# Which key tiles VectorE masks alone in a four-layer graph attention stack: second, sixth and eighth in place of third, sixth and eighth

## The chip, the cores and the metric

The kernel runs on one core of one Trainium2 chip. The metric is the device time of one execution in microseconds; the time before is the median of three runs.

## What is computed

The input is `x` of shape 16 x 1024 x 128 and one adjacency matrix of 1024 x 1024, with about one entry in 64 set. Three transformer layers follow each other and then one graph attention layer. One of the three, cut to what matters here:

```
Q, K, V = h @ Wq, h @ Wk, h @ Wv              # 8 heads of 16
scores  = Q K^T / sqrt(16); where adj == 0: -inf
attn    = softmax(scores) V
x = layer_norm(h + attn @ Wo + bo)
x = layer_norm(x + relu(x @ W1 + b1) @ W2 + b2)
```

The last layer adds a source and a destination score per edge, applies a leaky ReLU, masks, takes the softmax, sums the neighbours, adds the residual and normalises. The change touches only how the scores of the first three layers are masked.

## The kernel before, in words

**Blocks and steps.** A block is one batch element in one of the first three layers; there are 48, taken in groups of four batch elements (LANES, L655). A block has four *halves*: a group of four heads (g) and 512 of the queries (qh). A half has eight steps, one for each key tile of 128 keys, kt 0 to 7 in the code. So a block has 32 steps; they are numbered 0 to 31 below, and kt is the step modulo 8. The second, third, sixth and eighth key tile are kt 1, 2, 5 and 7.

**One step (score_step, L415).** TensorE computes the scores of two head pairs (pp 0 and 1), each into a PSUM buffer "s" of 128 x 1024 f32, of which there are three. Then each pair is masked and exponentiated, in one of two ways:

- The GpSimd way: ScalarE takes the exponential from PSUM into the tile `e` (L430), and GpSimd multiplies it by a 0/1 mask (L431). ScalarE frees the PSUM buffer.
- The VectorE way: VectorE adds a large negative number where there is no edge, from PSUM into `e` (L433), and ScalarE takes the exponential in place (L445). VectorE frees the PSUM buffer.

Pair 1 always goes the VectorE way. Pair 0 goes the GpSimd way, except at the key tiles in BOTH_ON_DVE (L37), where both go the VectorE way:

```
on_pool = pp == 0 and kt not in BOTH_ON_DVE
...
if on_pool:
    nc.scalar.activation(ev, psv, AF.Exp, scale=HD ** -0.5)
    behind["pool"] = nc.gpsimd.tensor_mul(ev, ev, m).ins
else:
    behind["dve"] = nc.vector.tensor_add(ev, psv, m).ins
    masked.append((2 * step_no[0] + pp + (kt not in BOTH_ON_DVE), ev))
```

A step of the second kind is called a *double step* below, and the others *mixed steps*. The list `masked` sets where ScalarE's in-place exponentials stand in its order (exponentials, L441): pair 0 of a double step in the same step, pair 1 of any step in the next one, behind that step's L430 if it is a mixed step.

**Four steps later (AHEAD, L36)** TensorE sums the values with `e` as weights into one PSUM buffer `acc` (av_step, L447; matmuls L450). With the last key tile of a half, which is summed in step 3 of the next half, finish (L453) transposes `acc` on VectorE into `tt` (L461). The first sum of the next half, in the step after, waits for that transposition, since `acc` has one buffer.

**The pieces.** All else is cut into pieces, at most one a step, put behind the step's scores and sums (piece, L691): the projections of the next block, and the output projection and feed-forward part of the block before. The table AT (L34) names the step of each piece. Pieces share one PSUM buffer "t". The second feed-forward product of the block before stands at steps 0 and 8, its output projection at 12 and 22; behind each of these come on VectorE an addition (L329), four bn_stats (L322) and four bn_aggr (L324), and on GpSimd the normalisation (L337 to L341). The splits of the projected keys and queries into a high and a low part (L385 on ScalarE, L386 on VectorE) stand at steps 9, 11, 14 and 17, the values' projection at 19 and 20. After the third layer of a batch element the pieces of the last layer (last_tasks, L541) ride in the same way, with edges (L607 on TensorE, L610 on VectorE) using the "s" buffers too.

**Orders.** In the main loop (L763) the order on TensorE and ScalarE is the program's own. On VectorE and GpSimd a planner orders the instructions ahead of time, by priority (the program's order, moved forward where soon(), L277, stands) among those that its own timing takes as ready; it also deals out the PSUM buffers. The transfers of SyncE are not touched by the change.

Of the kernel before, what the change touches and what calls it, by code (L numbers as in the profile page):

```python
# [33 lines left out]
AT = {"proj": (3, 6, 9, 11, 14, 17, 19, 20), "post": (12, 22, 23, 25, 26, 27, 28, 30, 32, 40, 41)}  # L34
AT_END = {3: (12, 21, 22, 24, 25, 26, 27, 28, 30, 31), 2: (8, 9, 13, 14, 15, 16, 17, 18, 20, 21)}
AHEAD = 4  # L36
BOTH_ON_DVE = (2, 5, 7)  # L37
TILES = {"w": 10, "x": LANES + 1, "last": 2}
BLOCKED = -57344.0

# [75 lines left out]
def fast_path(ctx: ExitStack, tc: tile.TileContext, a: dict, out: bass.AP, flag):  # L116
# [298 lines left out]
    def score_step(step):  # L415
# [3 lines left out]
        for pp in range(2):  # L419
# [6 lines left out]
            psv = ps.rearrange("p (r q) -> p r q", q=512)  # L426
            on_pool = pp == 0 and kt not in BOTH_ON_DVE
            m = (mask01 if on_pool else mask_add)[:, kt, q0:q0 + 512][:, None, :].to_broadcast([P, 2, 512])
# [3 lines left out]
# [3 lines that stand above are left out]
        step_no[0] += 1  # L435
# [616 lines left out]
```

## Time and profile before

| | |
|---|---|
| median of three runs | 3985.54 us (3984.45 to 3985.72) |
| the profiled execution's own time | 3983.09 us |
| its span, first to last instruction | 3981.2 us |
| mean granted TensorE clock | 0.987 |
| VectorE masks (L433) | 2112 of 1213 ns, 2493.6 us busy |
| ScalarE exponentials in place (L445) | 2112 of 1060 ns |
| ScalarE exponentials from PSUM (L430) | 960 of 1022 ns |
| GpSimd masks (L431) | 960 of 2026 ns |

A row of the timeline gives the start in microseconds, the busy time of the merged group, engine, line, operation, tiles written and read, and the count; a bracket at the end gives the engine's idle time ahead of it and what ended it. A row of the waits gives who waited for whom, the total in microseconds, the number of waits and the longest.

Measured from the first score matmul of one block to that of the next, 30 of the 48 blocks take 73.1 to 73.2 us and repeat the same pattern; they are called *plain blocks*. Most of the others carry pieces of the last layer and take 77 to 102 us; the first takes 82.5 us.

### The profile page before, as it was taken

How to read it: one execution, taken by the hardware profiler on the slowest of the kernel's cores; microseconds unless marked ns; L12 is line 12 of the kernel's file. 1: busy time of each engine (PE TensorE's matmuls, PEld its weight loads, DVE VectorE, ACT ScalarE, POOL GpSimd, SP SyncE). 2: the span in 40 equal slices, each digit the busy share in tenths (PEclk: the TensorE clock that was granted, in tenths of full speed). 3: DMA queues.
4: the chain of work that ended last, by engine and by line, in shares of the span. 5: the costliest groups of instructions: out<-in, count | busy, mean ns of one | idle time of the engine just before them, and what ended most of it. 6: DMA issues, size and time to landing. Idle time of an engine off the chain costs nothing.

```text
span 3981.2 us, 107823 instructions
## 1 busy us (share of the span) xinstructions
PE 3758.5 (94%) x44501; PEld 1558.5 (39%) x44501; DVE 3408.3 (86%) x5326; ACT 3392.8 (85%) x3961; POOL 3331.4 (84%) x3010
## 2 busy tenths in 40 slices
PE   7999999999999999999999999999999999999996
PEld 2333333344443333334444333333444433333345
DVE  7888988988888988988888898888888898898874
ACT  7999999977779999997777999999777799999860
POOL 4788888987789888988778888888877898898875
PEclk8999999999999999999999999999999999999998
DMA  6222222112222222222222222221222212222200
GB/s 163 65 65 53 55 65 63 46 48 65 56 58 57 65 65 54 54 65 55 55 55 55 65 53 56 65 64 45 55 55 55 71 46 62 65 51 58 66 8 20
DMA packets 124465, 233.13 MB, mean 59 GB/s; under 512 B 34624, under 2 KB 73792, under 8 KB 123968
## 3 DMA queue, kind: packets, MB, share of 16 engines
q1 hardware_dynamic: 123056, 225.74, 22.5%
q8 instruction: 354, 5.80, 0.6%
q14 instruction: 143, 1.17, 0.1%
q10 hardware_dynamic: 912, 0.42, 0.0%
HBM read 15.54 MB, written 8.39 MB: 6 GB/s over the span
## 4 chain that ended last, share of the span: by engine, by line
PE 61%; DVE 22%; POOL 9%; ACT 4%; issue 3%; SPq 0%; DMA 0%; DVEq 0%; ACTq 0%; POOLq 0%
PE acc L450 23%; PE t L297 19%; PE s L423 16%; DVE e L433 13%; POOL e L431 3%; POOL x L341 2%; PE t L286 2%; DVE lo L386 2%; DVE st L322 2%; ACT e L445 2%; ACT e L430 2%; DVE tt L461 1%; POOL mv L339 1%; PE s L297 1%; POOL x L345 1%
## 5 line engine op out<-in xcount | busy, mean ns | idle before, releaser
L433 DVE TENSOR_TENSOR e<-s,mask_add 128x1024 f32<-128x1024 f32 x2112 | 2493.6, 1213 | 344.6 <-PE s L423 263.7
L445 ACT ACTIVATE e<-e 128x1024 f32<-128x1024 f32 x2112 | 2203.4, 1060 | 206.1 <-DVE e L433 187.9
L431 POOL TENSOR_TENSOR e<-e,mask 128x1024 f32<-128x1024 f32 x960 | 1933.5, 2026 | 419.0 <-ACT e L430 419.0
L450 PE MATMUL acc<-e,v 128*17 128x512 f32 x12288 | 1627.8, 601 | 73.3 <-DVE tt L461 47.8
L423 PE MATMUL s<-Wq,Wk 64*128 64x512 f32 x6144 | 1185.0, 456 | 58.1 <-DVE e L433 41.3
L430 ACT ACTIVATE e<-s 128x1024 f32<-128x1024 f32 x960 | 980.8, 1022 | 227.5 <-PE s L423 226.5
L423 PEld LDWEIGHTS s<-Wq,Wk 64*128 64x128 f32 x6144 | 501.2, 185 | 1027.9 <-DVE e L433 417.1
L450 PEld LDWEIGHTS acc<-e,v 128*17 128x17 f32 x12288 | 208.6, 95 | 582.1 <-issue 452.0
L341 POOL TENSOR_SCALAR x<-x,mv 128x128 f32<-128x128 f32 x896 | 389.1, 447 | 23.5
L345 POOL TENSOR_TENSOR x<-x,ln_g 128x1024 f32<-128x1024 f32 (+1 forms) x97 | 229.5, 2367 | 25.1 <-PE t L286 22.6
L339 POOL TENSOR_TENSOR mv<-mv,half_neg 128x4 f32<-128x4 f32 x224 | 232.4, 1038 | 18.6
L297 PE MATMUL t<-hd,e 128*32 128x129 f32 x7040 | 208.2, 275 | 1.2
L329 DVE TENSOR_TENSOR x<-t,x 128x512 f32<-128x512 f32 x191 | 130.8, 685 | 86.9 <-PE t L297 86.9
L297 PEld LDWEIGHTS t<-hd,e 128*32 128x32 f32 x7040 | 194.6, 110 | 16.0 <-issue 5.0
L322 DVE BATCH_NORM_STATS2 st<-x 128x6 f32<-128x128 f32 x896 | 197.3, 280 | 3.3
L297 PE MATMUL t<-x1T,W 128*32 128x512 f32 x1520 | 198.0, 592 | 0.0
L297 PEld LDWEIGHTS t<-W,hT 128*32 128x32 f32 x6080 | 170.0, 110 | 58.5 <-issue 45.5
L297 PE MATMUL t<-W,hT 128*32 128x128 f32 x6080 | 183.4, 273 | 0.2 <-DVE x L625 0.2
L286 PE MATMUL t<-identf,x 128*128 128x128 f32 x872 | 151.0, 289 | 34.0 <-DVE lo L386 15.4
L286 PEld LDWEIGHTS t<-identf,x 128*128 128x128 f32 x872 | 92.9, 141 | 230.2 <-issue 108.3
L337 POOL TENSOR_SCALAR mv<-mv 128x4 f32<-128x4 f32 x224 | 53.0, 236 | 124.6 <-DVE mv L324 98.8
L610 DVE SCALAR_TENSOR_TENSOR e<-s,mask 128x1024 f32<-128x1024 f32 x128 | 150.3, 1214 | 5.9 <-PE s L607 5.0
(118 smaller groups left out, 2573.9 us busy)
## 6 DMA issues: line engine op xcount, KB each, us to landing
Wk<-hi SPq DMA_DIRECT2D x384, 128.0 KB
Wk<-lo SPq DMA_DIRECT2D x384, 128.0 KB
Wq<-hi SPq DMA_DIRECT2D x384, 128.0 KB
Wq<-lo SPq DMA_DIRECT2D x384, 128.0 KB
x<-in_x_dram SPq DMA_DIRECT2D x16, 512.0 KB
out_dram<-x SPq DMA_DIRECT2D x31, 256.0 KB
ai<-in_adj_dram SPq DMA_DIRECT2D x8, 512.0 KB
g_rows<-parts SPq DMA_DIRECT2D x124, 4.0 KB
```

Source lines behind the costliest of these rows:

```text
L286: nc.tensor.transpose(ps[:, t * P:(t + 1) * P], src[:, 4 * h + t, :], identf)
L297: nc.tensor.matmul(dst[j:j + SLOT, :], lhsT[:, j:j + SLOT], rhs, start=start, stop=stop)
L322: nc.vector.bn_stats(st[:, t, :], z[:, t, :])
L339: nc.gpsimd.tensor_tensor(v, v, half_neg[:, ts], OP.pow)
L341: nc.gpsimd.tensor_scalar(z[:, t, :], z[:, t, :], mv[:, t, 0:1], mv[:, t, 1:2], op0=OP.add, op1=OP.mult)
L345: nc.gpsimd.tensor_mul(z, z, rows(gain, n))
L423: nc.tensor.matmul(ps[:, r * 512:(r + 1) * 512], k[64 * r:64 * r + 64, kt * P:(kt + 1) * P], q[64 * r:64 * r + 64, q0:q0 + 512], start=Tru ...
L430: nc.scalar.activation(ev, psv, AF.Exp, scale=HD ** -0.5)
L431: behind["pool"] = nc.gpsimd.tensor_mul(ev, ev, m).ins
L433: behind["dve"] = nc.vector.tensor_add(ev, psv, m).ins
L445: nc.scalar.activation(ev, ev, AF.Exp, scale=HD ** -0.5)
L450: nc.tensor.matmul(acc[j * SLOT:j * SLOT + HD + 1, :], v_bufs[m % 2][:, kt, 2 * j + g, :], e[:, j, :], start=first, stop=last)
```

## The change

VectorE takes both pairs of kt 1 in place of kt 2. The numbers of instructions of every kind stay as they are.

```diff
-BOTH_ON_DVE = (2, 5, 7)
+BOTH_ON_DVE = (1, 5, 7)
```

## The prediction

> **What bounds the kernel now.** I read the page's busy times first, then the waits, then the timeline of one plain block, engine by engine.
>
> ```profile
> PE 3758.5 (94%) x44501; PEld 1558.5 (39%) x44501; DVE 3408.3 (86%) x5326; ACT 3392.8 (85%) x3961; POOL 3331.4 (84%) x3010
> ```
>
> Four engines are nearly full, TensorE the most. A bare step (scores and sums, no piece) takes 1.64 us on TensorE when nothing is late (scores at 1416.32 and 1417.97 below). In that time ScalarE has two exponentials to issue (about 0.95 us apart, 1.9 us), and VectorE one mask (1.13 us apart when back to back) or two (2.3 us). So VectorE and ScalarE are behind in bare stretches and catch up where pieces lengthen the step; only lateness beyond the three "s" buffers reaches TensorE. What it waits for:
>
> ```profile
> PE acc L450 <- DVE tt L461: 47.8, 84, 1.0
> PE s L423 <- DVE e L433: 41.3, 108, 0.9
> PE acc L450 <- POOL e L431: 16.0, 15, 1.7
> ```
>
> The largest wait is that of a half's first sum for the transposition of the half before. Three of the four transpositions of a plain block are late, at steps 4, 12 and 20, by 0.31, 0.65 and 0.56 us (sum start against score start plus 0.66 us): 1.5 us x 30 blocks is about the 47.8 us. One plain block (it starts at 1367.59) from step 17 to step 21, on ScalarE, VectorE and TensorE:
>
> ```profile
> 1408.43 1.06 ACT L445 ACTIVATE e<-e 128x1024 f32<-128x1024 f32 x1
> 1409.38 0.59 ACT L385 CAST hi<-t 128x512 fp32r<-128x512 f32 x1
> ```
>
> ```profile
> 1405.08 3.49 DVE L433 TENSOR_TENSOR e<-s,mask_add 128x1024 f32<-128x1024 f32 x3
> 1409.61 1.22 DVE L433 TENSOR_TENSOR e<-s,mask_add 128x1024 f32<-128x1024 f32 x1 [1.04 <-PE s L423]
> 1410.76 0.68 DVE L386 TENSOR_TENSOR lo<-t,hi 128x512 fp32r<-128x512 f32 x1
> 1411.35 2.35 DVE L433 TENSOR_TENSOR e<-s,mask_add 128x1024 f32<-128x1024 f32 x2
> 1413.62 0.71 DVE L461 STREAM_TRANSPOSE tt<-acc 128x512 f32<-128x512 f32 x1
> ```
>
> ```profile
> 1413.18 0.73 PE L423 MATMUL s<-Wq,Wk 64*128 64x512 f32 x4
> 1414.47 1.05 PE L450 MATMUL acc<-e,v 128*17 128x512 f32 x8 [0.56 <-DVE tt L461]
> ...
> 1416.32 0.73 PE L423 MATMUL s<-Wq,Wk 64*128 64x512 f32 x4
> 1416.98 1.05 PE L450 MATMUL acc<-e,v 128*17 128x512 f32 x8
> 1417.97 0.73 PE L423 MATMUL s<-Wq,Wk 64*128 64x512 f32 x4
> ```
>
> ScalarE takes step 17's split (L385) right behind its exponentials, without a wait. On VectorE the group of three at 1405.08 ends with the only mask of step 17. VectorE then sits idle for 1.04 us until step 18's scores, and from there has two masks of step 18 (the double step), a split (L386) and the mask of step 19 in one row, so that the transposition starts at 1413.62, though the sums it reads are done about 1.33 us after their start (1411.32), at 1412.65: at another half's end, where VectorE is free, it starts 1.33 us after. TensorE loses 0.56 us.
>
> **What the Trainium skill says.** "PSUM — Partial Sum Buffer", section "Engine vs sequencer instructions": the queues of ScalarE, VectorE and GpSimd are strict FIFO. The trace agrees: L461 above stands 0.97 us behind ready work. "VectorE: DVE Perf Modes", section "The TRN2 errata — SBUF-src ops pay a fixed extra latency per instruction": an fp32 tensor_tensor takes (N+151)/0.96 ns; for N = 1024 that is 1224 ns, and the trace has 1213 for the mask, which reads one operand from PSUM. "Perfetto Trace Analysis", section "Identifying the Most-Contended Engine": matmul busy time is no good measure of headroom; here too I go by idle gaps and step lengths, not by the 94%.
>
> **The change, step by step.** Nothing is added or removed: 2112 masks on VectorE (1213 ns), 960 on GpSimd (2026 ns) and 3072 exponentials stay. In each half one mask moves from kt 2 to kt 1 on VectorE, one from kt 1 to kt 2 on GpSimd, and ScalarE's order at kt 1 becomes: pair 1 of kt 0, pair 0 of kt 1, then the piece's work. No DMA moves. I work out each half of a plain block; times are from the block's first score matmul.
>
> *Third half (steps 17, 18).* Step 17's two masks now run at 39.76 and 40.89, the second in the idle 1.04 us. ScalarE exponentiates step 17's pair 0 at 40.98 in place of L430 at 39.93, and reaches L385 at about 41.9 as before (41.79), so L386 can run at 42.55 in place of 43.18. From 42.1 VectorE has L386 (0.6), one mask of step 18 and one of step 19 (1.13 each) ahead of L461: 42.55 + 0.65 + 1.13 + 1.13 = 45.5, against 46.04. It ends at 46.2, plus 0.14 until the matmul starts: 46.34; TensorE by itself would be there at 46.27. **Gain 0.55 us.** Next late there is TensorE itself.
>
> *First half (steps 1, 2).* Step 1's masks meet the addition and statistics (L329, L322, L324) of the piece at step 0. Where the planner puts them is the question that decides most. The trace has both cases:
>
> ```profile
> 1371.23 0.69 DVE L329 TENSOR_TENSOR x<-t,x 128x512 f32<-128x512 f32 x1 [1.16 <-PE t L297]
> 1371.96 0.87 DVE L322 BATCH_NORM_STATS2 st<-x 128x6 f32<-128x128 f32 x4
> 1372.75 0.36 DVE L324 BATCH_NORM_AGGREGATE mv<-st 128x2 f32<-128x6 f32 x4
> 1373.03 4.59 DVE L433 TENSOR_TENSOR e<-s,mask_add 128x1024 f32<-128x1024 f32 x4
> ```
>
> ```profile
> 1398.32 0.69 DVE L329 TENSOR_TENSOR x<-t,x 128x512 f32<-128x512 f32 x1 [0.22 <-PE t L297]
> 1398.92 1.21 DVE L433 TENSOR_TENSOR e<-s,mask_add 128x1024 f32<-128x1024 f32 x1
> 1400.06 0.86 DVE L322 BATCH_NORM_STATS2 st<-x 128x6 f32<-128x128 f32 x4
> ```
>
> The first is step 1, a mixed step: statistics first. The second is step 13, a double step: its pair 0 is ready when L329 ends and slips in ahead. Over the trace L329 is followed by a mask in 47 of 47 cases at step 13, 37 of 37 at step 23 and 9 of 9 at kt 2, all double steps, and by L322 in all 82 at steps 1 and 9 and in 3 of 4 at step 31, a double step too (I went through VectorE's instructions in order of time). So I take pair 0 of step 1 at 4.25, statistics at 5.4, pair 1 at 6.45 and step 2's mask at 7.55. Step 2's second scores wait 0.1 us for pair 0 (free at 5.5); step 3's scores start at about 7.7 and 8.0 in place of 6.72 and 7.81, its sums at 8.2 to 8.4 against 8.24; L461 starts at 9.85 against 9.94. **Gain 0.1 us**, give or take 0.15.
>
> *Second half (steps 9, 10).* Same meeting. VectorE is busy without a gap from 20.92 to 30.5, and with the same four masks ahead of L461 stays so: L329 20.92, pair 0 at 21.53, statistics, pair 1 at 23.74, L386 24.87, masks 25.47 and 26.6, L461 27.73 against 27.89. ScalarE reaches step 11's L430 at 26.1 as before (26.11). **Gain 0.15 us.**
>
> *Fourth half (steps 25, 26).* Its transposition isn't late, and ScalarE reaches L506 at 62.8 as before. **Nothing**; what hides the moved mask is VectorE's slack of about 0.6 us there, and a mask over that would cost at most 1.1 us.
>
> *GpSimd* now has kt 2, 3 and 4 in a row, 6.1 us of masks. In plain blocks each ends at least 1 us ahead of its sum, four steps later (step 26's at about 68.3 against 69.65), so I take 0. In the blocks where step 23 waits for the mask of step 19 (1.7 us by the timeline), GpSimd would idle until step 17's statistics and start its row of normalisation and scaling up to 0.85 us later: 0 to 0.85 us on six blocks, 0 to +5 us in all.
>
> *The other 18 blocks* have the third half's pattern in part (about half show a late step 20): -0.55 to +0.3 each; I take -0.2. The first block's step 1, where VectorE's order is written out, gets a mask more: at most 1.2 us once, which I leave out.
>
> **Sum.** -(0.55 + 0.1 + 0.15) = -0.8 a plain block; I take -0.75, x 30 = -22.5; -0.2 x 18 = -3.6: -26 us against the profiled execution's 3983.09 us, which lies 2.45 us under the median of the runs. On the median: 3985.5 - 26 = 3960.
>
> **Rivals.**
> - *Slower: the statistics go ahead of the double step's masks.* For it: at steps 1 and 9 they do now, and 3 of 4 double steps at 31. Against it: the 93 cases above. Then step 1's pair 0 is masked at 5.44, step 2's second scores wait until 6.69 (1.28 us), and ScalarE has one more exponential (0.95) in the row it works off without a gap from 6.66 to 21.3: +0.77. In the second half ScalarE idles from 22.3 to 23.9, and step 12's piece comes about 1.0 us later. With the third half's gain: 0.77 + 1.0 - 0.55 = +1.2 x 30 = +37 us: 4022. It decides once pair 0 at step 1 starts after about 5.0; with one of the two meetings lost it is -0.55 + 0.8 = +0.25 a block, +8 us.
> - *Same: the gain at step 20 is taken back.* If step 19's second scores wait for step 18's ScalarE exponential (43.4, +0.3 us), or GpSimd's row of three costs its +5 us and the small gains of the first two halves fail: -0.3 x 30 + 5 = -4 us: 3981.
>
> **How the numbers follow.** Forecast 3960 with its neighbours (its own range 3945 to 3976): 0.50. Taken back: 0.14. Slower: 0.36. A difference under about 0.2% (8 us) can't be told from none. The low end takes 1.2 us on every plain block (all of step 20, half of 12 and 4, 36 us and 4 more elsewhere). The high end goes to the slower rival's 4022.
>
> **What would show it.** Right: the wait of L450 for tt falls from 47.8 to about 25 us; VectorE's gap ahead of step 18 is gone; at steps 1 and 9 one L433 stands between L329 and L322; plain blocks take 72.4 us. Wrong: L322 directly behind L329 at step 1; TensorE's wait for L433 at kt 2 and 3 above 41.3 us; a wait for L431 far above 16 us.

## The result

| | before | changed |
|---|---|---|
| median | 3984.99 us (3979.72 to 3985.72, 4 runs) | 3958.11 us (3957.37 to 3960.06, 4 runs) |
| profiled execution | 3983.09 us, span 3981.2 | 3958.22 us, span 3956.1 |
| plain block, median | 73.15 us | 72.48 us |

The ratio is 0.9936, with a 95% interval of 0.9919 to 0.9953: faster by 0.6%, or 26.9 us between the medians, against the 26 us forecast. The page's first line and TensorE's largest waits after the change:

```profile
PE 3770.4 (95%) x44501; PEld 1552.3 (39%) x44501; DVE 3407.3 (86%) x5326; ACT 3371.7 (85%) x3961; POOL 3329.4 (84%) x3010
```

```profile
PE s L423 <- DVE e L433: 29.2, 85, 1.7
PE acc L450 <- DVE tt L461: 23.0, 87, 1.3
PE t L286 <- DVE lo L386: 19.6, 19, 1.5
PE s L423 <- ACT e L430: 17.8, 37, 0.5
...
PE acc L450 <- POOL e L431: 8.3, 12, 0.7
```

The instructions are the same, and no engine's busy time moved by as much as 0.7% (ScalarE has 21 us less). The wait for the transposition fell from 47.8 to 23.0 us. Sorted by step, it is gone at step 20 (20.4 us before) and at step 12 it fell from 20.3 to 6.5. At step 4 it rose from 6.2 to 13.9, but 8.4 us at step 4 had been put down to GpSimd's L341 before. The waits for VectorE's and GpSimd's masks fell too. One wait is new: 17.8 us for ScalarE's exponential from PSUM (it was 0.7). Nearly all of it, 17.3 us, stands at step 3.

Steps 17 to 20 of the same plain block (it starts at 1359.65 now), on VectorE, ScalarE, TensorE and, as PEld, TensorE's loading of weights ahead of its matmuls:

```profile
1396.84 4.61 DVE L433 TENSOR_TENSOR e<-s,mask_add 128x1024 f32<-128x1024 f32 x4
1401.61 1.23 DVE L433 TENSOR_TENSOR e<-s,mask_add 128x1024 f32<-128x1024 f32 x1 [0.16 <-PE s L423]
1402.75 0.68 DVE L386 TENSOR_TENSOR lo<-t,hi 128x512 fp32r<-128x512 f32 x1
1403.47 1.23 DVE L433 TENSOR_TENSOR e<-s,mask_add 128x1024 f32<-128x1024 f32 x1
1404.61 0.71 DVE L461 STREAM_TRANSPOSE tt<-acc 128x512 f32<-128x512 f32 x1
```

```profile
1401.84 1.03 ACT L430 ACTIVATE e<-s 128x1024 f32<-128x1024 f32 x1
```

```profile
1402.41 1.02 PE L423 MATMUL s<-Wq,Wk 64*128 64x512 f32 x4
...
1405.22 0.73 PE L423 MATMUL s<-Wq,Wk 64*128 64x512 f32 x4
1405.88 1.05 PE L450 MATMUL acc<-e,v 128*17 128x512 f32 x8
```

```profile
1402.92 0.19 PEld L423 LDWEIGHTS s<-Wq,Wk 64*128 64x128 f32 x2 [0.32 <-ACT e L430]
```

The group of masks at 1396.84 has grown from three to four: both of step 17 are in it, and VectorE's idle time ahead of step 18 is 0.16 us in place of 1.04. Between there and L461 stand two masks and the split, not three masks and the split, and the sums of step 20 follow their scores after 0.66 us, with no wait. But the score group of step 19 takes 1.02 us in place of 0.73: its second pair waits for the PSUM buffer that ScalarE's L430 of step 18 frees at 1402.87, as the last line shows. (The list of waits above counts matmuls alone, so this one isn't in its 17.8 us.)

Step 1, VectorE:

```profile
1363.20 0.69 DVE L329 TENSOR_TENSOR x<-t,x 128x512 f32<-128x512 f32 x1 [1.09 <-PE t L297]
1363.81 1.21 DVE L433 TENSOR_TENSOR e<-s,mask_add 128x1024 f32<-128x1024 f32 x1
1364.94 0.86 DVE L322 BATCH_NORM_STATS2 st<-x 128x6 f32<-128x128 f32 x4
```

Pair 0's mask stands between the addition and the statistics, as it did at step 13. Over the whole trace that holds in 37 of 37 cases at step 1 and 45 of 45 at step 9.

The difference of the spans, 25.1 us, split by the starts of the score matmuls (changed less before; over the plain blocks, means for the halves and medians for the steps):

| where | us |
|---|---|
| first half of a plain block | -0.06 (step 2 +0.73, step 3 -0.86, step 7 +0.15) |
| second half | -0.25 (step 11 +0.11, step 12 -0.38) |
| third half | -0.36 (step 19 +0.26, step 20 -0.62) |
| fourth half | +0.01 |
| 29 plain blocks | -19.2 |
| the other 19 blocks | -5.2 (first halves -2.1, second -0.9, third -6.3, fourth +4.0) |
| ahead of the first step and behind the last | -0.7 |

(There are 29 plain blocks, not the 30 that the text ahead of the result counts: the second block takes 71.7 us.)

The other blocks need care. In the plain blocks the granted clock of TensorE is 1.00 in every trace read here. In the others it falls in places, and not in the same blocks from trace to trace. The first half of one of them (at 1127.8 us) takes 26.44 us in the trace before, at a granted clock of 0.94, and 25.53 us at 1.00 in that of a kernel below that leaves first halves as they were. So a few microseconds on these blocks, the first halves' -2.1 above all, can come from the clock and not from the change.

### The profile page after: what moved, and what is told of

The parts are those of the page before. It is cut to its first block, busy times and chain, and to the rows that moved or that the text cites. A ratio compares the mean times of both kernels' runs of the same rounds, so it can differ in the third digit from the quotient of the medians.

```text
span 3956.1 us, 107747 instructions
## 1 busy us (share of the span) xinstructions
PE 3770.4 (95%) x44501; PEld 1552.3 (39%) x44501; DVE 3407.3 (86%) x5326; ACT 3371.7 (85%) x3961; POOL 3329.4 (84%) x3010
## 4 chain that ended last, share of the span: by engine, by line
PE 66%; DVE 26%; POOL 3%; issue 3%; ACT 1%; SPq 0%; DMA 0%; DVEq 0%; POOLq 0%; ACTq 0%
PE acc L450 24%; PE t L297 20%; PE s L423 18%; DVE e L433 16%; DVE st L322 3%; PE t L286 2%; DVE tt L461 1%; DVE lo L386 1%; DVE mv L324 1%; POOL e L431 1%; PE s L297 1%; PE s L607 1%; DVE x L329 1%; POOL x L345 1%; DVE e L610 1%
## 5 line engine op out<-in xcount | busy, mean ns | idle before, releaser
L423 PE MATMUL s<-Wq,Wk 64*128 64x512 f32 x6144 | 1198.1, 458 | 62.1 <-DVE e L433 29.2
L430 ACT ACTIVATE e<-s 128x1024 f32<-128x1024 f32 x960 | 982.4, 1023 | 168.9 <-PE s L423 168.8
L341 POOL TENSOR_SCALAR x<-x,mv 128x128 f32<-128x128 f32 x896 | 389.7, 449 | 23.5
L286 PE MATMUL t<-identf,x 128*128 128x128 f32 x872 | 150.5, 288 | 33.5 <-DVE lo L386 19.6
```

Source lines behind the costliest of these rows:

```text
L286: nc.tensor.transpose(ps[:, t * P:(t + 1) * P], src[:, 4 * h + t, :], identf)
L341: nc.gpsimd.tensor_scalar(z[:, t, :], z[:, t, :], mv[:, t, 0:1], mv[:, t, 1:2], op0=OP.add, op1=OP.mult)
L423: nc.tensor.matmul(ps[:, r * 512:(r + 1) * 512], k[64 * r:64 * r + 64, kt * P:(kt + 1) * P], q[64 * r:64 * r + 64, q0:q0 + 512], start=Tru ...
```

## The experiments

The theory: VectorE's work between step 18's scores and the transposition set step 20, and moving one mask ahead of those scores, into idle time, took it off that path. At step 12, where VectorE has no idle time, the new order makes the row ahead of the transposition a little shorter. The main rivals: that the gain lies in the planner's new order as a whole, or in the place of the mask for another engine's sake; and, for the prediction's slower case, the price of statistics ahead of masks.

**One half at a time.** Four kernels, each with the double step at kt 1 in one half only:

```diff
-BOTH_ON_DVE = (2, 5, 7)
+BOTH_ON_DVE = ((2, 5, 7), (2, 5, 7), (1, 5, 7), (2, 5, 7))   # here the third half
...
-        e = e_tile()
+        e, both = e_tile(), BOTH_ON_DVE[2 * g + qh]
...
-            on_pool = pp == 0 and kt not in BOTH_ON_DVE
+            on_pool = pp == 0 and kt not in both
...
-                masked.append((2 * step_no[0] + pp + (kt not in BOTH_ON_DVE), ev))
+                masked.append((2 * step_no[0] + pp + (kt not in both), ev))
```

> Only the third half of each block (steps 16 to 23) has the double step at kt 1; the others keep kt 2. Theory (VectorE's idle microsecond at step 17 takes over a mask that otherwise delays the transposition that step 20 waits for): plain blocks 0.36 us shorter, all of it at steps 19 and 20 (19 later by 0.27, 20 shorter by 0.62); about -10 us on the plain blocks and -6 us on the others, some -16 us in all. Rival (the gain comes from the planner's new order as a whole, so a part of the change alone need not bring a part of it): any other number, for example within 3 us of before.

> Only the second half (steps 8 to 15) has the double step at kt 1. Theory (no ScalarE-bound split between the masks ahead of the transposition for step 12): plain blocks 0.25 us shorter, at step 12; -7 to -8 us in all. Rival (the planner's order as a whole): not -5 to -11 us.

> Only the first half (steps 0 to 7) has the double step at kt 1. Theory (its pair 0 slips in ahead of the statistics, and the wait moves from step 3 to step 2): plain blocks 0.06 us shorter, step 2 later by 0.73 and step 3 sooner by 0.86; -2 to -4 us in all. Rival (the statistics come first when only this half moves): +0.7 us a block, +20 to +35 us.

> Only the fourth half (steps 24 to 31) has the double step at kt 1. Theory (nothing waits for its transposition): plain blocks unchanged to 0.02 us; between 0 and +5 us in all, since the blocks with pieces of the last layer lost 4 us in this half. Rival (each double step at kt 1 brings its share): about -6 us.

| half moved alone | ratio to before (95%) | its own half in a plain block, us | 29 plain blocks, us | other blocks, us |
|---|---|---|---|---|
| third | 0.9953 (0.9937 to 0.9970) | -0.35 (step 19 +0.27, step 20 -0.63) | -10.2 | -12.8 |
| second | 0.9976 (0.9967 to 0.9985) | -0.24 (step 12 -0.39) | -6.8 | -3.6 |
| first | 1.0010 (1.0003 to 1.0017) | +0.03 (step 2 +0.80, step 3 -0.86) | -0.3 | +3.3 |
| fourth | 1.0013 (1.0006 to 1.0019) | +0.01 (the next block's first half -0.09) | -2.1 | +4.4 |

The third half alone brings the larger part of the gain, at the steps named, and the second half most of the rest. The first half was expected to gain 2 to 4 us and is 0.1% slower: a miss, small. The fourth half was to leave the plain blocks as they were to 0.02 us; its own steps stay, but in 28 of the 29 plain blocks the first half, which follows the fourth half of the block before, is about 0.1 us shorter. In the plain blocks the four totals sum to -19.4 us against -19.2 for the whole change: there the halves add up. For the other blocks the sum (-8.7 against -5.2) decides nothing: 5.1 of the 12.8 us of the third half's kernel lie in first halves, which it doesn't touch and where the granted clock differs. The waits in the kernel with the third half alone:

```profile
PE s L423 <- DVE e L433: 44.6, 118, 0.9
PE acc L450 <- DVE tt L461: 27.6, 48, 1.0
```

The wait for the transposition falls by 20 us and no other falls with it as far.

**The same path shortened without moving a mask.** The kernel before, with its double steps at kt 2, but the piece with the last split (TensorE's projection, ScalarE's L385 and VectorE's L386) a step earlier:

```diff
-AT = {"proj": (3, 6, 9, 11, 14, 17, 19, 20), ...
+AT = {"proj": (3, 6, 9, 11, 14, 16, 19, 20), ...
```

> The kernel before with its double steps as they were, but the piece at step 17 (the last split of the queries) put at step 16, so that its 0.68 us on VectorE lies ahead of the idle microsecond and not between the masks and the transposition. Theory (what stands between step 18's scores and the transposition sets when step 20's sums start, whatever it is): the transposition for step 20 starts 0.4 to 0.6 us sooner, the sums of step 20 are no longer late by 0.56 us, plain blocks are 0.2 to 0.5 us shorter. Rival (it is the place of the mask as such, for GpSimd's or ScalarE's sake): step 20 still waits, plain blocks within 0.1 us of before or longer.

The ratio to before is 0.9966 (0.9954 to 0.9979). VectorE from step 17 in the plain block (it starts at 1361.71), and TensorE's wait for the transposition:

```profile
1402.26 0.69 DVE L386 TENSOR_TENSOR lo<-t,hi 128x512 fp32r<-128x512 f32 x1 [0.71 <-ACT hi L385]
1402.87 4.61 DVE L433 TENSOR_TENSOR e<-s,mask_add 128x1024 f32<-128x1024 f32 x4
1407.39 0.70 DVE L461 STREAM_TRANSPOSE tt<-acc 128x512 f32<-128x512 f32 x1
```

```profile
PE acc L450 <- DVE tt L461: 27.7, 52, 1.0
```

Here the split goes first, ahead of the only mask of step 17, and VectorE waits 0.71 us for ScalarE's part of it; behind it four masks stand in one row. Ahead of step 18 it had waited 1.04 us. So a third of a microsecond less is lost, and the transposition starts as much sooner: 45.68 us into the block, against 46.02 before. The third half of a plain block is 0.36 us shorter and the wait for the transposition is 27.7 us, both as in the kernel with the mask moved in that half alone (0.35 and 27.6). So no mask has to change its step or its engine for this gain; it is enough that the transposition starts sooner. In both kernels step 20 gains 0.6 us, and the steps ahead of it give about 0.25 us back. The test has a flaw: TensorE's part of the piece moved too, so that step 16 is 0.54 us longer and step 17 1.02 us shorter.

**A spare mask in the idle time.** Meant as a direct test of the idle microsecond: the pair 1 mask of step 17 is issued twice, in both kernels.

```diff
-                behind["dve"] = nc.vector.tensor_add(ev, psv, m).ins
+                for _ in range(2 if (g, qh, kt, pp) == (1, 0, 1, 1) else 1): behind["dve"] = nc.vector.tensor_add(ev, psv, m).ins
```

> The kernel before, with the pair 1 mask of step 17 in the third half done twice over (same operands, same result): 1.13 us more VectorE work a block, set into its idle 1.04 us. Theory (that idle time is free): plain blocks longer by 0 to 0.1 us, under 5 us in all. Rival (VectorE's work as such is the bound, at 86% of the span): 1.1 us a block, about +50 us.

> The changed kernel with the same spare mask at step 17, where VectorE now has no idle time. Theory (the idle time was what the change used): the transposition for step 20 comes 1.1 us later, so plain blocks are 0.8 to 1.1 us longer than with the change alone, 3985 to 4010 us in all, and the gain is gone. Rival (the gain doesn't rest on that idle time): within 5 us of the changed kernel.

In the kernel before it costs 0.38 us in a plain block (ratio to before 1.0047, 1.0031 to 1.0064); in the changed kernel 0.45 us (ratio to before 1.0009, 1.0001 to 1.0018, so the gain is gone, though nearly half of the loss, 11.9 us, lies in the other blocks). In a plain block it was to be under 0.1 and over 0.8 us, so neither theory's numbers came; the second kernel's total of 3988 us lies in the range given for it. VectorE and TensorE in the first of the two, steps 17 to 20:

```profile
1412.18 4.75 DVE L433 TENSOR_TENSOR e<-s,mask_add 128x1024 f32<-128x1024 f32 x4
1417.10 0.69 DVE L386 TENSOR_TENSOR lo<-t,hi 128x512 fp32r<-128x512 f32 x1 [0.17 <-ACT hi L385]
1417.70 3.47 DVE L433 TENSOR_TENSOR e<-s,mask_add 128x1024 f32<-128x1024 f32 x3
```

```profile
1418.97 0.50 PE L423 MATMUL s<-Wq,Wk 64*128 64x512 f32 x2 [0.72 <-DVE e L433]
```

The spare mask waits for the one whose output it writes again (1.26 us apart, not 1.13), ends 0.2 us after step 18's scores are there, and now the split goes ahead of step 18's masks, so that TensorE waits 0.72 us at step 19 for the buffer of the first of them. In the changed kernel the transposition had ended 0.4 us ahead of the sums of step 20, which swallowed a part of the 0.85 us by which the spare mask delayed it. About half of its 0.45 us comes in another way: step 19's first scores now wait 0.43 us for the buffer that ScalarE's exponential of step 18 frees, and step 20's scores come 0.23 us later. The pair doesn't tell the theories apart, since in both kernels the order or the buffers behind the spare mask changed with it.

**The slower rival, forced.** The changed kernel, with pair 0 of steps 1 and 9 ordered behind the statistics:

```diff
-            nc.vector.bn_aggr(mv[:, t, :], st[:, t, :])
+            behind["stats"] = nc.vector.bn_aggr(mv[:, t, :], st[:, t, :]).ins
...
-                behind["dve"] = nc.vector.tensor_add(ev, psv, m).ins
+                with tc.issue_after(behind["stats"]) if g == 0 and kt == 1 and pp == 0 and "stats" in behind else nullcontext(): behind["dve"] = ...
```

> The changed kernel, with pair 0 of the double steps 1 and 9 ordered on VectorE behind the last bn_aggr of the piece before. Theory of the prediction's slower rival: step 2's second scores wait until 6.7 us, step 12's piece comes 1 us later: +0.8 us a plain block in the first half and +1.2 in the second against the changed kernel, plain blocks about 74.4 us, some 4015 to 4025 us in all. Other theory (the order of masks and statistics hardly matters, since the sum of VectorE's work ahead of the transposition is the same): within 8 us of the changed kernel, 3950 to 3966 us.

4062.28 us; the ratio to before is 1.0198 (1.0181 to 1.0215). Step 1 in a plain block (it starts at 1394.49):

```profile
1398.04 0.69 DVE L329 TENSOR_TENSOR x<-t,x 128x512 f32<-128x512 f32 x1 [1.10 <-PE t L297]
1398.77 0.87 DVE L322 BATCH_NORM_STATS2 st<-x 128x6 f32<-128x128 f32 x4
1399.55 0.36 DVE L324 BATCH_NORM_AGGREGATE mv<-st 128x2 f32<-128x6 f32 x4
1399.84 3.45 DVE L433 TENSOR_TENSOR e<-s,mask_add 128x1024 f32<-128x1024 f32 x3
```

```profile
1401.08 0.50 PE L423 MATMUL s<-Wq,Wk 64*128 64x512 f32 x2 [1.04 <-DVE e L433]
```

Step 2's second scores start 6.59 us into the block (the prediction's case had 6.69). Against the changed kernel a plain block loses 0.79 us in the first half, as expected, and 1.96 in the second, where 1.2 was expected. There the planner also put three masks ahead of the split of step 9, where the changed kernel has two, so its second half holds more than the edit meant. At step 1, where the edit does what it says, it is worth 0.79 us a block whether a mask or eight small instructions of 1.1 us together go first: more than the 0.66 us of the whole change.

**Better than both?** Step 0 carries 64 small matmuls, and VectorE idles behind them until the addition is ready (1.09 us in the changed kernel's lines above). So: the first half's double step at kt 0; then combinations.

```diff
-BOTH_ON_DVE = (1, 5, 7)
+BOTH_ON_DVE = ((0, 5, 7), (1, 5, 7), (1, 5, 7), (1, 5, 7))   # i1
+BOTH_ON_DVE = ((2, 5, 7), (1, 5, 7), (1, 5, 7), (2, 5, 7))   # i3
+BOTH_ON_DVE = ((0, 5, 7), (1, 5, 7), (1, 5, 7), (2, 5, 7))   # i4
+BOTH_ON_DVE = ((0, 5, 7), (0, 5, 7), (1, 5, 7), (2, 5, 7))   # i5
```

> The changed kernel with the first half's double steps at kt 0, 5 and 7: step 0 carries a piece of 64 small matmuls, behind which VectorE idles for about 1 us before the addition of the piece is ready. Theory (a double step belongs where VectorE idles for TensorE's sake): the stall of 0.73 us at step 2 goes and plain blocks get 0.5 to 0.9 us shorter than with the change, 3930 to 3945 us in all. Rival (two double steps in a row, 31 and 0, exceed the three PSUM buffers): 0.5 to 1 us longer, 3970 to 3990 us.

> The double step at kt 1 in the second and third half only, where it gained; first and fourth as before. Theory (the halves add up): plain blocks 0.6 us shorter than before (-17 us on all of them), and -10 to -16 us on the others: 3950 to 3957 us, 2 to 8 us below the changed kernel. Rival (they don't add up on the other blocks): no different from the changed kernel.

> First half at kt 0, second and third at kt 1, fourth at kt 2. Theory: the 0.64 us that kt 0 gained in the first half, less the 0.40 us that the late GpSimd mask of step 14 cost at step 18, and without the fourth half's loss on the other blocks: 3942 to 3952 us. Rival (GpSimd's lateness grows): not below the kernel with the second and third half alone.

> First and second half at kt 0, third at kt 1, fourth at kt 2. Theory: VectorE has no idle time at step 8, so kt 0 there only delays the transpositions of the gathered heads and gains nothing over kt 1: 3942 to 3960 us, not below the same kernel with kt 1 in the second half. Rival (a piece of 64 matmuls hides a double step wherever it stands): 5 us or more below it.

| | ratio to before (95%) | span, us | plain block by half, less before, us |
|---|---|---|---|
| changed kernel | 0.9936 (0.9919 to 0.9953) | 3956.1 | -0.06, -0.25, -0.36, +0.01 |
| i1 | 0.9928 (0.9912 to 0.9945) | 3948.0 | -0.70, -0.19, +0.04, +0.03 |
| i3 | 0.9927 (0.9914 to 0.9940) | 3956.7 | 0, -0.24, -0.36, +0.02 |
| i4 | 0.9907 (0.9893 to 0.9922) | 3946.0 | -0.67, -0.21, +0.01, +0.01 |
| i5 | 0.9905 (0.9890 to 0.9919) | 3940.5 | -0.66, -0.58, +0.41, +0.02 |

i1 came short of its 0.5 to 0.9 us a block (0.14 in all): the first half gains 0.64 us over the changed kernel, but 0.40 is lost in the third half, which wasn't touched. TensorE in i1 at step 18 (block start 1357.78), then its waits:

```profile
1399.68 1.05 PE L450 MATMUL acc<-e,v 128*17 128x512 f32 x8 [0.64 <-POOL e L431]
```

```profile
PE acc L450 <- POOL e L431: 29.8, 44, 1.1
...
PE acc L450 <- DVE tt L461: 10.5, 26, 0.9
```

The sums of step 18 wait for the GpSimd mask of step 14: GpSimd has become the bound there. The profile shows it idle for 3.42 us ahead of its first mask in this block, since step 0 gives it none. i3 is no different from the changed kernel within the interval. i4 (3947.0 us) and i5 (3945.7 us) are the fastest, about 1% below before, each within what was expected. In i5 that is luck: kt 0 was to gain nothing in the second half, where it gains 0.37 us more than i4, and the third half loses 0.40, again to GpSimd's wait (42.2 us over the run). The two can't be told apart. Their intervals reach to the edge of the changed kernel's, so the size of the step beyond it (11 to 12 us by the medians) is not sharp; their 8 runs (3942.3 to 3951.4) all lie below its 4.

## Why the prediction was right

**Third half: right in place, too large.** Step 20 gained 0.62 us (forecast 0.55, from a wait of 0.56). 0.26 of it went back at step 19, where the second scores wait for ScalarE's exponential of step 18: the take-back named as a rival, at its 0.3 us, though not enough of it to undo the gain. The failed term is the claim that TensorE itself would be next late at step 20: step 19 was. L461 started at 44.96, not at 45.5, since the planner put step 18's mask ahead of the split; that made no difference to step 20.

**Second half: right, too small.** 0.25 for 0.15. In the kernel with this half alone the transposition starts at 27.65, where 27.73 was forecast and 27.89 was before.

**First half: the number came by luck.** It is 0.06 for 0.1, inside the margin given. But alone, that half gets 0.03 us longer, and the kernel with the fourth half alone has 0.09 us less in the first half that follows. The two sum to the 0.06 of the changed kernel, so the gain comes from a half for which the forecast had nothing; why it comes there isn't shown. What was said of the order holds: step 2's second scores came at 5.42 (forecast 5.5). Step 3's came at 7.43 and 7.76 in place of 7.7 and 8.0, because the first of them took the buffer that ScalarE freed at 7.37. So the wait at step 3 moved from its second scores, for VectorE, to its first, for ScalarE, and step 2 got longer by it. Step 7 lost 0.15 us, which the forecast hadn't: its second scores now wait for ScalarE's exponential of step 6.

**Fourth half:** nothing in its own steps of the plain blocks, as forecast. On the other blocks the fourth halves cost 4 to 6 us, for which the sum had no term of its own.

**The order of masks and statistics** was the step on which the sign hung. Reading it from the 93 double steps of the trace before, and not from what stands at steps 1 and 9 themselves, was right in every case. The price of the other order was underestimated: 4022 us was forecast and 4062 measured, with the planner's further change counted in.

**The sum:** -0.66 us a plain block for -0.75, on 29 blocks for 30: -19.2 for -22.5. The other blocks brought -5.2 for -3.6, part of which can be the clock, and there is 0.7 at the ends that wasn't in the sum. -25 us against -26: two errors of 2 to 3 us cancel in part, and that it came so close is luck.

**The reading of the wait.** The prediction took the 47.8 us for the three late transpositions of 30 plain blocks, 1.5 us each. Sorted by step, 16.6 us of it stand at step 12 and 16.1 at step 20 of the plain blocks, and 15.0 in the other blocks. The lateness at step 4 isn't in it: the profile puts that down to GpSimd's L341. The forecast of about 25 us (23.0 came) so held in its main part, step 20, and by luck in the rest.

**GpSimd's three masks in a row** cost nothing that shows: the wait for its masks fell from 16.0 to 8.3 us. For the six blocks where up to 0.85 us of loss was feared, the lateness at step 23 fell, from 9.7 to 3.9 us in all (1.7 to 0.7 in one read closely), while step 18 got later by 0.8, TensorE's transposes waiting for the split L386 (19.6 us over the run for 15.4). In that block the statistics of a piece of the last layer do go ahead of step 17's masks, which puts the split behind all of them: the slower rival's order, at a place that the forecast hadn't looked at.

## What to carry to other kernels

When work is moved between steps and its amount stays, look for the wait that ends last after it and list what the queue holds between the last thing that releases that queue and the instruction waited for: what leaves that stretch counts, and what releases the queue sooner. Where a planner sets an order, take it from places in the trace with the same circumstances, and price the other order, since it can be worth more than the edit. Here the gains of the four halves added up in the plain blocks; in i1 and i5 they didn't, since the next engine (GpSimd at step 18) took a part back, as ScalarE did at step 19 in the changed kernel. A part of the gain can also show in a stage next to the one changed, so test the parts one by one before you call a term right.

## What the runs showed beyond that

A repeated mask that writes the output of the one just ahead of it started 1.26 us after it, where independent masks start 1.13 us apart: four in a row took 4.75 us in place of 4.61.
